# Softmax attention in layer 2: scores by halves, each followed by its banks of maxima

## The chip, the cores and the metric

The kernel runs on one core of a Trainium2 chip. The metric is device time in microseconds (us) of one execution. The engines are called as in the profile: PE is TensorE's matmuls, PEld its weight loads, DVE is VectorE, ACT is ScalarE, POOL is GpSimd and SP is SyncE. PSUM, where matmuls put their results, has eight banks of 512 float32 columns on each of 128 partitions.

## What is computed

The program is a chain of four layers on an array `x` of 2 sequences x 1024 positions x 128 features. Each layer has the form

```python
xn = _layernorm(x, axis=-1)
s = attention_of_the_layer(xn, ...)
g = _silu(ffn_of_the_layer(xn, ...))
x = x + s * g
```

The change is inside the feed-forward branch of layer 2, which itself starts with a causal softmax attention (16 query heads of 8 dimensions, 4 groups of key and value heads, so 4 query heads share one key head):

```python
scores = jnp.einsum('bghsd,bgtd->bghst', Q, K) / jnp.sqrt(jnp.float32(D_K))
mask = jnp.triu(jnp.full((S, S), -1000000000.0, dtype=scores.dtype), k=1)
attn = jax.nn.softmax(scores + mask, axis=-1)
out = jnp.einsum('bghst,bgtd->bghsd', attn, V)
```

A mixture of experts follows it, and layers 0, 1 and 3 hold state-space, delta-rule and expert work that the change leaves alone.

## The kernel before

**Tiling.** A sequence of 1024 is cut into 8 tiles of 128 positions. `steps` lists all pairs of a query tile `sb` and a key tile `tb <= sb` for both sequences: 2 x 36 = 72 steps, numbered from 0. Steps with `tb == sb` are the diagonal ones and need the causal mask. The four head groups lie on the four row groups of the array: group g uses partitions 32g to 32g+31 (`kT[rows]`, `qT[rows]`), so a score matmul contracts over 32 rows, and four of them, one for each group, can stand in the array side by side. Work that uses all 128 rows (the mask matmuls, `pat`, transposes) needs the whole array.

**What a step computes** (`weights`, line 1559). For each group, one matmul writes scores of 128 keys x (4 heads x 128 queries), that is one bank of 512 columns. A second matmul adds the "shift", the negated maximum of each query, kept transposed in `mT`, by multiplying it with ones. In a diagonal step a full-width matmul of `ident` and `nle` puts the mask in first. Groups 0 and 1 share one tile of two banks (`psc`), groups 2 and 3 another. One ACT instruction takes Exp of such a pair of banks into `pr`. A step later `values` multiplies `pr` with the values `va` into the bank `pat`: four matmuls that the profile shows as eight.

**Maxima** (`maxima`, line 1523). The shifts have to exist before a query tile's first step. So every step also computes "banks of maxima" for a later query tile: a tile `pm` of one bank gets scores with queries on the partitions (1 matmul of 512 or 384 columns, 2 of 256, or 4 of 128), and one DVE `tensor_reduce` takes the maxima of it (`mx`). A "masked" bank covers the diagonal keys of one group: a full-width mask matmul (`nge`) first, then 4 matmuls of 128 columns. A "plain" bank needs no mask. `largest` joins the parts into `mp`, `turn` transposes it on PE (`pmt`) and casts it to `mT`. `take` hands out so many banks a step that each tile is done when it is due. By its arithmetic, steps 0 to 37 have five banks (nearly all one masked and four plain), steps 38 to 51 four, 52 to 61 three plain ones, and 62 to 71 none.

**Closing.** When a query tile is done, `close` schedules three small parts into later steps: four transposes of `ao` and a normalisation (`rec`, `at`), one transpose (`patT`), one projection (`pho`). Parts of the next stage (`hidden_columns`, `group_logits`) are put in the same way. All these use `pm` banks and stand at the front of a step.

**Buffers.** The pool `sm` has three banks for `pm` and the small parts, `sc` two tiles of two banks for `psc`, `so` one for `pat`.

**Order.** PE's order in this stage is exactly as written (`manual_schedule` for PE). The other engines' instructions are put in order by the framework's planner, from a model of the time. The written order of one step is:

1. small parts that are due (`run`);
2. mask matmuls of the masked banks (`whole(before)`), and in a diagonal step the `nle` masks of all four groups (the part of `weights` up to its `yield`);
3. the score matmuls of the list `before` (masked banks, filled up with plain ones taken from the end of the step's list, up to three), one matmul of each bank in turn (`rows`);
4. four score matmuls, then four shift matmuls, then the two Exps;
5. the banks of the list `after` (up to three);
6. `values` of the step before.

In a five-bank step with the usual lists that is one masked bank and the plain bank of group 3 ahead of the scores, and the plain banks of groups 0, 1 and 2 behind them.

Every matmul is issued by the helper `K.mm` (line 319), so the profile gives line 319 for all of them, and their tiles tell them apart: `psc<-qT,kT` is a score, `psc<-mT,onesR` a shift, `psc<-nleR,identR` a mask of the step, `pm<-ngeR,identR` the mask of a masked bank, `pm<-kT,qT` a bank of maxima, `pat<-pr,va` the values. `pr<-psc` at line 291 is Exp, `mx<-pm` at line 1535 the reduction.

Of the kernel before, what the change touches and what calls it, by code (L numbers as in the profile page):

```python
# [10 lines left out]
F32 = mybir.dt.float32  # L11
# [8 lines left out]
P = 128  # L20
# [1192 lines left out]
class Dispatch:  # L1213
# [93 lines left out]
    def weights(self, dst, n, rows):  # L1307

        nc = self.K.nc
        e = nc.values_load(self.of[0:1, n : n + 1], engines=[mybir.EngineType.SP], min_val=0, max_val=self.E - 1, skip_runtime_bounds_check_because="a count of experts, at most E - 1")  # L1310
        nc.sync.dma_start(dst, rows[bass.ds(e, 1)].rearrange("e p m -> p (e m)"))
# [122 lines left out]
class Attention:  # L1434
# [73 lines left out]
    def maxima(self, sb, shared, sm):  # L1508

        K, pf, qT, kT = self.K, self.pf, self.qT, self.kT
        nc = K.nc
        four = [P, G, P]
        now = slice(sb * P, (sb + 1) * P)
        mp = shared["mp"][(self.b * TPB + sb) % 4]
        banks = self.banks(sb)
        starts = sorted({a for a, *_ in banks})
        mx = pf.tile([P, len(starts), 4, 4], F32, name=f"mx{len(starts)}", bufs=3)

        def bank(a, m, j, k, g, masked):
            tile = []

            def mask():
                tile.append(sm.tile([P, 512], F32, name="pm", tag="pm"))
                K.mm(tile[0], shared["ident"], shared["nge"], True, False)

            def scores():
                if not masked:
                    tile.append(sm.tile([P, 512], F32, name="pm", tag="pm"))  # L1530
                rows = slice(32 * g, 32 * g + 32)
                for jj in range(k):
                    K.mm(tile[0][:, jj * m : (jj + 1) * m], qT[rows, j + jj, now], kT[rows, a : a + m], not masked, jj == k - 1 or not masked)
                    yield
                nc.vector.tensor_reduce(mx[:, starts.index(a), g, j : j + k], tile[0][:, : k * m].rearrange("p (j m) -> p j m", m=m), AX.X, ALU.max)  # L1535

            return (mask if masked else None), scores

        def largest():
            top = mx[:, 0]  # L1540
            for n in range(1, len(starts)):
                new = pf.tile([P, 4, 4], F32, name="top", bufs=2)
                nc.vector.tensor_max(new, top, mx[:, n])
                top = new
            top = top.rearrange("p g j -> p j g")
            m = mp.rearrange("p j (g r) -> p j g r", r=32)
            nc.vector.tensor_scalar_mul(m[:, :, :, 0], top, -1.0)
            nc.vector.scalar_tensor_tensor(m[:, :, :, 1], top, -1.0, m[:, :, :, 0].bitcast(F32), ALU.mult, ALU.subtract)

        def turn():  # L1550
            pt = sm.tile(four, F32, name="pmt", tag="pm")
            for j in range(4):
                K.mm(pt[:, j, :], mp[:, j, :], shared["ident"])
            self.mT[sb] = pf.tile(four, F32R, name="mT", bufs=4)
            nc.scalar.copy(self.mT[sb], pt)

        return [bank(*b) for b in banks if b[-1]], [bank(*b) for b in banks if not b[-1]], largest, turn

    def weights(self, sb, tb, shared, sc):

        K, qT, kT = self.K, self.qT, self.kT
        scale = float(np.float32(1.0) / np.sqrt(np.float32(8.0)))
        now = slice(sb * P, (sb + 1) * P)
        pair = [P, 2, 4, P]
        psc = [sc.tile(pair, F32, name="psc", tag="ps") for _ in range(2)]
        bank = lambda g: psc[g // 2][:, g % 2]
        rows = lambda g: slice(32 * g, 32 * g + 32)
        if tb == sb:
            for g in range(4):
                K.mm(bank(g), shared["ident"], shared["nle"], True, False)  # L1570
        yield
        for g in range(4):
            K.mm(bank(g), kT[rows(g), tb * P : (tb + 1) * P], qT[rows(g), :, now], tb < sb, False)
        for g in range(4):
            K.mm(bank(g), shared["ones"][rows(g), :], self.mT[sb][rows(g), :, :], False, True)
        self.pr = []
        for ps in psc:
            pr = self.loop.tile(pair, F32, name="pr", bufs=4)
            K.act(pr, ps, AF.Exp, scale=scale)
            self.pr += [pr[:, 0], pr[:, 1]]  # L1580

    def values(self, sb, tb, prs, so):
        if tb == 0:
# [37 lines left out]
def softmax_attention(K, pf, sm, sc, so, seqs, fill):  # L1621

    nc, c = K.nc, K.c
    four = [P, G, P]

    shared = {n: pf.tile(s, F32R, name=n + "R") for n, s in (("ident", [P, P]), ("ones", [P, P]), ("nge", four), ("nle", four))}
    nc.vector.tensor_copy(shared["ident"], c["ident"])
    nc.vector.tensor_copy(shared["ones"], c["ones"])  # L1630
    for n in ("nge", "nle"):
        nc.vector.tensor_copy(shared[n], seqs[0].w[n].unsqueeze(1).to_broadcast(four))
    shared["mp"] = [pf.tile(four, F32R, name=f"mp{n}") for n in range(4)]
    for t in shared["mp"]:
        nc.vector.memset(t.bitcast(F32), 0.0)
    tiles = [(b, sb) for b in range(NB) for sb in range(TPB)]
    steps = [(b, sb, tb) for b, sb in tiles for tb in range(sb + 1)]
    first = [steps.index((b, sb, 0)) for b, sb in tiles]
    plan = []
    for n, (b, sb) in enumerate(tiles):  # L1640
        plan.append(dict(zip(("masked", "plain", "largest", "turn"), seqs[b].maxima(sb, shared, sm))))
        plan[-1]["due"] = first[n] - (2 if n < 3 else 3)
    later = {}
    for s, part in fill:
        later.setdefault(s, []).append(part)

    def take(kind, s, most):

        want = left = 0
        for p in plan:  # L1650
            left += len(p[kind])
            if left:
                want = max(want, -(-left // max(1, p["due"] - s + 1)))
        out = []
        while len(out) < min(want, most):
            p = next(p for p in plan if p[kind])
            out.append(p[kind].pop(0))
        for n, p in enumerate(plan):
            if p["largest"] and not p["masked"] and not p["plain"]:
                ready.append((n, p))  # L1660
        return out

    ready = []

    def run(parts):
        for t in parts:
            if isinstance(t, dict):
                t["turn"]()
                t["turn"] = None
            else:  # L1670
                t()

    def whole(units):
        for full, _ in units:
            if full:
                full()

    def rows(units):
        live = [r() for _, r in units]
        while live:  # L1680
            live = [r for r in live if next(r, r) is not r]

    def finish(s):

        for n, p in ready:
            if p["largest"]:
                assert n < 4 or plan[n - 4]["turn"] is None
                p["largest"]()
                p["largest"] = None
                later.setdefault(max(s + 1, first[n] - 1), []).append(p)  # L1690
        ready.clear()

    def phase(units):
        for a in range(0, len(units), 3):
            whole(units[a : a + 3])
            rows(units[a : a + 3])

    for s in range(-4, 0):
        run(later.pop(s, ()))
        phase(take("masked", s, 99))  # L1700
        phase(take("plain", s, 99))
        finish(s)
    last = None
    for s, (b, sb, tb) in enumerate(steps):
        A = seqs[b]
        before = take("masked", s, 3)
        after = take("plain", s, 6)
        run(later.pop(s, ()))
        room = 3 - len(before)
        extra = after[3:]  # L1710
        after = after[:3]
        before += extra[:room]
        after += extra[room:]
        whole(before)
        w = A.weights(sb, tb, shared, sc)
        next(w)
        rows(before)
        next(w, None)
        rows(after[:3])
        rows(after[3:])  # L1720
        finish(s)
        if last:
            last()

        def last(A=A, s=s, sb=sb, tb=tb, prs=A.pr):
            A.values(sb, tb, prs, so)
            if tb == sb:
                for n, part in enumerate(A.close(sb, sm)):
                    later.setdefault(s + 3 + n, []).append(part)

    last()
    for s in sorted(later):
        run(later[s])
# [211 lines left out]
```

## Time and profile before

| | |
|---|---|
| median of 3 runs | 1346.4 us (1341.18 to 1348.06) |
| the profiled execution's own time | 1351.32 us |
| its span, first to last instruction | 1349.5 us |
| mean granted PE clock over the span | 0.91 |
| PE / DVE / ACT busy in the span | 1154.1 / 870.4 / 507.2 us |
| this stage: first bank of maxima to last Exp | 503.8 to 817.8 us |
| score matmuls / shift matmuls / Exps | 288 / 288 / 144 |
| reductions of maxima | 304 |

Durations in the text come from the profiled execution, whose own time is 4.9 us above the median. In a timeline line the first number is the start in us from the span's start, the second the length of the merged group, `xN` its number of instructions, and square brackets give the engine's idle time before it and what ended it. A line that merges several instructions gives the shape of the first.

### The profile page before, as it was taken

Reading aid. Unit: us, or ns where it says so; the run is one execution under the profiler, and the core shown is the slowest. Engines: PE = TensorE matmul, PEld = TensorE weight load, DVE = VectorE, ACT = ScalarE, POOL = GpSimd, SP = SyncE. Lnnn points to the kernel's source line nnn. Section 1 sums busy time; section 2 is a strip of 40 time slices with the busy share of each in tenths; the row PEclk is TensorE's granted clock in tenths of the full one; section 3 lists DMA queues with packets and bytes.
Section 4 is the critical chain, followed back from the end, with each engine's and each line's share of the span. In section 5 each row is a group of like instructions: output and inputs, shape, how many; then the busy total and the mean of one; then the engine's idle time right before and its main releaser. Section 6 shows DMA issues by size and latency. Waiting matters only on the chain. (4 is left out here: it accounts for less than half of the span.)

```text
span 1349.5 us, 18601 instructions
## 1 busy us (share of the span) xinstructions
PE 1154.1 (86%) x6697; PEld 773.1 (57%) x6697; DVE 870.4 (64%) x2260; ACT 507.2 (38%) x919; POOL 389.9 (29%) x386
## 2 busy tenths in 40 slices
PE   5599977888999288999998995899999378999996
PEld 2267665886996145444444432577778353554555
DVE  7944368946756966777777735877765582363447
ACT  4533335123222241454555674144242244522221
POOL 0073530056642520000000000244775120635430
PEclk9799987899999585999999997799999768999998
DMA  2000003035443000000000000233445311222201
GB/s 90 1 0 1 1 15 125 27 127 156 126 122 97 8 1 0 1 0 1 1 1 17 9 1 8 93 112 117 133 124 142 95 70 33 45 53 62 45 18 32
DMA packets 37803, 71.26 MB, mean 53 GB/s; under 512 B 5275, under 2 KB 22176, under 8 KB 37328
## 3 DMA queue, kind: packets, MB, share of 16 engines
q1 hardware_dynamic: 31408, 55.09, 13.7%
q0 software_dynamic: 5440, 9.79, 3.0%
q10 hardware_dynamic: 864, 5.20, 1.1%
q8 instruction: 53, 0.87, 0.3%
q14 instruction: 38, 0.31, 0.1%
HBM read 62.58 MB, written 8.85 MB: 53 GB/s over the span
## 5 line engine op out<-in xcount | busy, mean ns | idle before, releaser
L1305 POOL DMA_INDIRECT xb<-xs,dfrom x85 | 84.4, 993 | 505.3 <-PE pcum L319 359.7
L1535 DVE TENSOR_REDUCE mx<-pm 128x1 f32<-128x512 f32 (+3 forms) x304 | 181.9, 656 | 63.0 <-PE pm L319 60.5
L291 ACT ACTIVATE pr<-psc 128x1024 f32<-128x1024 f32 x144 | 139.5, 1021 | 99.7 <-PE psc L319 72.6
L319 PE MATMUL pm<-kT,qT 32*128 32x128 f32 (+3 forms) x576 | 119.6, 364 | 15.5 <-DVE mx L1535 11.7
L1315 POOL DMA_INDIRECT ys<-yb,dto x85 | 87.4, 1028 | 82.0 <-DVE yb L1202 50.5
L319 PEld LDWEIGHTS pm<-kT,qT 32*128 32x128 f32 x576 | 69.5, 203 | 69.0 <-DVE mx L1535 48.7
L319 PE MATMUL p<-xbT,tw 128*128 128x256 f32 x368 | 99.3, 386 | 3.8 <-ACT sg L1195 2.6
L325 PE MATMUL tp<-w_c,xn 128*128 128x128 f32 x64 | 20.2, 408 | 72.6 <-DVE xn L369 45.7
L319 PE MATMUL pat<-pr,va 128*32 128x512 f32 x576 | 79.6, 619 | 0.2 <-ACT pr L291 0.2
L1195 ACT ACTIVATE sg<-p,tw 128x256 f32<-128x256 f32 x92 | 41.0, 471 | 91.9 <-PE p L319 74.3
L319 PEld LDWEIGHTS p<-xbT,tw 128*128 128x128 f32 x368 | 62.7, 192 | 14.6 <-ACT sg L1195 4.1
L319 PE MATMUL psc<-qT,kT 32*128 32x512 f32 x288 | 63.7, 487 | 2.8 <-ACT pr L291 2.7
L1196 DVE SCALAR_TENSOR_TENSOR hh<-p,tw,sg 128x256 f32<-128x256 f32 x92 | 42.5, 479 | 33.8 <-ACT sg L1195 22.4
L1875 POOL TENSOR_TENSOR hT<-hT,gb 128x512 f32<-128x512 f32 x32 | 41.2, 1291 | 72.0 <-DVE hT L1873 67.9
L319 PEld LDWEIGHTS po<-tw,hh 128*128 128x128 f32 x368 | 54.4, 192 | 9.3 <-issue 3.8
L1873 DVE TENSOR_TENSOR hT<-hT,put 128x512 f32<-128x512 f32 x36 | 24.5, 685 | 54.5 <-PE put L319 53.1
L325 PEld LDWEIGHTS tp<-w_c,xn 128*128 128x128 f32 x64 | 11.8, 190 | 80.3 <-ACT lnrs L291 46.4
L319 PE MATMUL po<-tw,hh 128*128 128x128 f32 x368 | 56.3, 277 | 0.5 <-DVE hh L1196 0.4
L319 PE MATMUL psc<-mT,onesR 32*128 32x512 f32 x288 | 53.6, 407 | 0.0
L291 ACT ACTIVATE hT<-pgt 128x512 f32<-128x512 f32 x36 | 21.4, 597 | 72.5 <-PE pgt L319 70.0
L605 POOL TENSOR_TENSOR uda<-w_c,vdA 128x512 f32<-128x512 f32 x28 | 28.6, 1039 | 62.4 <-PE pe L319 37.1
L646 DVE TENSOR_TENSOR uxdt<-pt,vdt 128x512 f32<-128x512 f32 x16 | 10.4, 684 | 48.0 <-PE pt L644 47.9
(522 smaller groups left out, 2756.4 us busy)
## 6 DMA issues: line engine op xcount, KB each, us to landing
tw<-in_rows SPq DMA_DIRECT2D x23, 836.0 KB
tw<-in_rows SPq DMA_DIRECT2D x39, 384.0 KB
gb<-gt SPq DMA_DIRECT2D x32, 256.0 KB
yt<-ys SPq DMA_DIRECT2D x16, 256.0 KB
w_l<-in_l ACTq DMA_DIRECT2D x1, 1890.0 KB
w_e<-in_e SPq DMA_DIRECT2D x1, 1536.0 KB
xb<-xs,dfrom POOLq DMA_INDIRECT x85
ys<-yb,dto POOLq DMA_INDIRECT x85
```

What stands on the lines that cost most here:

```text
L291: op = self.nc.scalar.activation(out, in_, func, **kw)
L319: self.nc.tensor.matmul(out, lhsT=lhsT, rhs=rhs, start=start, stop=stop)
L325: self.nc.tensor.transpose(pt[:, j, :], src(g * G + j), self.c["ident"])
L605: pool.tensor_mul(da, upto.unsqueeze(1).unsqueeze(1).to_broadcast(lay), m["dA"][:, i0 + j : i0 + j + per, :].unsqueeze(3).to_broadcast(lay))
L646: nc.vector.tensor_mul(heads(xdt[:, k]), heads(pt), each(m["dt"], k))
L1195: nc.scalar.activation(sg, p1[:, k - k0, :], AF.Silu, bias=t[:, 1536 + k : 1537 + k])
L1196: nc.vector.scalar_tensor_tensor(hh[:, k, :], p2[:, k - k0, :], t[:, 1540 + k : 1541 + k], sg, ALU.add, ALU.mult)
L1305: self.K.nc.gpsimd.indirect_dma_start(dst, None, self.xs, bass.IndirectOffsetOnAxis(self.of_token[:, n : n + 1], 0))
L1315: d = self.K.nc.gpsimd.indirect_dma_start(self.ys, bass.IndirectOffsetOnAxis(self.to[:, n : n + 1], 0), src, None, bounds_check=2 * T - 1, ...
L1535: nc.vector.tensor_reduce(mx[:, starts.index(a), g, j : j + k], tile[0][:, : k * m].rearrange("p (j m) -> p j m", m=m), AX.X, ALU.max)
L1873: nc.vector.tensor_mul(hT, hT, put)
L1875: nc.gpsimd.tensor_mul(hT, hT, gb[k // 2][:, k % 2, :])
```

## The change

`weights` does one half of the groups in a call: half 0 is groups 0 and 1, half 1 groups 2 and 3. A half is its masks (in a diagonal step), its two scores, its two shifts and its Exp. The written order of a step becomes: small parts; mask matmuls of the masked banks; half 0; up to three banks (the masked ones, filled up with plain ones); half 1; the other banks; `values` of the step before. Each unit now carries its group, and the plain banks are sorted so that those of groups 2 and 3 come first. Numbers of instructions, buffers and what `take` hands out stay as they were.

```diff
-            return (mask if masked else None), scores
+            return (mask if masked else None), scores, g
...
-    def weights(self, sb, tb, shared, sc):
+    def weights(self, sb, tb, shared, sc, half):
...
-        psc = [sc.tile(pair, F32, name="psc", tag="ps") for _ in range(2)]
-        bank = lambda g: psc[g // 2][:, g % 2]
+        psc = sc.tile(pair, F32, name="psc", tag="ps")
+        groups = (2 * half, 2 * half + 1)
         rows = lambda g: slice(32 * g, 32 * g + 32)
         if tb == sb:
-            for g in range(4):
-                K.mm(bank(g), shared["ident"], shared["nle"], True, False)
-        yield
-        for g in range(4):
-            K.mm(bank(g), kT[rows(g), tb * P : (tb + 1) * P], qT[rows(g), :, now], tb < sb, False)
-        for g in range(4):
-            K.mm(bank(g), shared["ones"][rows(g), :], self.mT[sb][rows(g), :, :], False, True)
-        self.pr = []
-        for ps in psc:
-            pr = self.loop.tile(pair, F32, name="pr", bufs=4)
-            K.act(pr, ps, AF.Exp, scale=scale)
-            self.pr += [pr[:, 0], pr[:, 1]]
+            for g in groups:
+                K.mm(psc[:, g % 2], shared["ident"], shared["nle"], True, False)
+        for g in groups:
+            K.mm(psc[:, g % 2], kT[rows(g), tb * P : (tb + 1) * P], qT[rows(g), :, now], tb < sb, False)
+        for g in groups:
+            K.mm(psc[:, g % 2], shared["ones"][rows(g), :], self.mT[sb][rows(g), :, :], False, True)
+        pr = self.loop.tile(pair, F32, name="pr", bufs=4)
+        K.act(pr, psc, AF.Exp, scale=scale)
+        self.pr = (self.pr if half else []) + [pr[:, 0], pr[:, 1]]
...
-        before = take("masked", s, 3)
-        after = take("plain", s, 6)
+        masked = take("masked", s, 3)
+        plain = take("plain", s, 6)
         run(later.pop(s, ()))
-        room = 3 - len(before)
-        extra = after[3:]
-        after = after[:3]
-        before += extra[:room]
-        after += extra[room:]
-        whole(before)
-        w = A.weights(sb, tb, shared, sc)
-        next(w)
-        rows(before)
-        next(w, None)
-        rows(after[:3])
-        rows(after[3:])
+        whole(masked)
+        plain.sort(key=lambda unit: unit[2] < 2)
+        room = 3 - len(masked)
+        A.weights(sb, tb, shared, sc, 0)
+        rows(masked + plain[:room])
+        A.weights(sb, tb, shared, sc, 1)
+        rows(plain[room : room + 3])
+        rows(plain[room + 3 :])
         finish(s)
```

The helpers `whole` and `rows` only unpack the third element of a unit.

## The prediction

> **What bounds the stage now.** The edit touches one stage, softmax attention in layer 2, so I first cut the span into stretches (the windows view), setting the borders by the Exp instructions in the timeline.
>
> ```profile
> 532.00:700.70 168.70, 160.86 (x1125) 80.64 (x1122) 127.36 (x252) 86.29 (x111) 0.00 (x0) 0.95 0.00 1
> 700.70:762.50 61.80, 56.22 (x432) 30.28 (x431) 45.94 (x97) 34.63 (x54) 0.00 (x0) 0.97 0.05 14
> 762.50:790.60 28.10, 27.40 (x225) 12.37 (x221) 19.96 (x44) 21.46 (x28) 0.00 (x0) 1.00 0.00 1
> 790.60:822.00 31.40, 27.26 (x188) 9.18 (x186) 2.08 (x6) 21.24 (x26) 0.00 (x0) 1.00 0.00 1
> ```
>
> Columns: length, busy PE, PEld, DVE, ACT, POOL, then clock. The stretches hold steps 0-37 (five banks of maxima each), 38-51 (four), 52-61 (three) and 62-71 (none). PE is nearly always busy, but overlapping matmuls count as busy, so I ask the waits view who stands still in steps 0-51:
>
> ```profile
> PEld pm L319 <- DVE mx L1535: 52.5, 107, 1.5
> DVE mx L1535 <- PE pm L319: 43.1, 46, 4.7
> ```
>
> Each waits for the other: a loop through the three `pm` banks, bound by its latency. One step of it, from the timeline (step 21, PE and then DVE):
>
> ```profile
> 629.68 0.50 PE L319 MATMUL pm<-ngeR,identR 128*128 128x512 f32 x1
> 630.11 0.50 PE L319 MATMUL pm<-kT,qT 32*128 32x128 f32 x2
> 630.12 0.49 PE L319 MATMUL psc<-qT,kT 32*128 32x512 f32 x1
> ...
> 630.46 0.40 PE L319 MATMUL psc<-mT,onesR 32*128 32x512 f32 x1
> ...
> 631.40 1.08 PE L319 MATMUL pm<-kT,qT 32*128 32x512 f32 x2
> 632.41 1.06 PE L319 MATMUL pat<-pr,va 128*32 128x512 f32 x8
> 633.41 0.50 PE L319 MATMUL pm<-ngeR,identR 128*128 128x512 f32 x1
> 630.65 3.08 DVE L1535 TENSOR_REDUCE mx<-pm 128x1 f32<-128x512 f32 x5 [0.66 <-PE pm L319]
> ```
>
> The loop: mask 0.43, first bank to first reduction 0.54 (630.11 to 630.65), two reductions 0.60 + 0.68 (the fifth bank needs the buffer of the second), 0.06 to the fifth bank, 0.41 to `pat`, 1.00 to the next mask: 3.73 us, the distance of the two masks. The eight score and shift matmuls lie under the two reductions.
>
> **Two facts about order.** The second line above shows a score of another row group starting 0.01 us after the first banks, though three masked matmuls stand before it in the written order: a group that is blocked doesn't hold up the others. Signals behave otherwise. Step 34:
>
> ```profile
> 680.50 0.39 PE L319 MATMUL psc<-mT,onesR 32*128 32x512 f32 x2
> ...
> 680.64 0.44 PE L319 MATMUL psc<-qT,kT 32*128 32x512 f32 x1
> ...
> 681.20 1.94 ACT L291 ACTIVATE pr<-psc 128x1024 f32<-128x1024 f32 x2 [1.58 <-PE pm L319]
> ```
>
> Here the masked bank is in group 2, so the shifts of groups 0 and 1, all that the first Exp reads, end at 680.50 + 0.39 = 680.89. The Exp starts at 681.20. What ends at 681.08 is the score of group 2, which stands ahead of those shifts in the written order. In step 21 the last shift itself ends at 631.28 and Exp starts at 631.38, also 0.10 later. I read this as: a matmul's completion is seen only when all written before it have completed.
>
> **Part 1, half 0 moves ahead of the maxima (29 five-bank steps without the diagonal).** New order: mask, scores 0 and 1, shifts 0 and 1, three banks, half 1, two banks, `pat`. The sort puts groups 2 and 3 first, so those banks start beside half 0. But their signals wait for shift 1: score to shift 0.34 (630.12 to 630.46), shift 0.39, reduction 0.04 later (641.36 + 0.44 for a bank, reduction at 641.84): 0.77 instead of 0.54. The loop grows by 0.23. It is not 0.23 everywhere. With 384 columns the second reduction is now another 384-wide one and costs 0.47 instead of the masked bank's 0.60, leaving 0.23 - 0.13 = 0.10. Where DVE is still occupied by `top`, `mp`, `rec` and `at`, or the masked bank is in group 3 (first reduction already 0.65 late), I take 0.05. Sum: 8 x 0.23 + 9 x 0.10 + 12 x 0.05 = +3.3 us; bounds 0 and 29 x 0.23 = +6.7.
> Half 1 (scores, shifts) costs nothing while it lies under the two reductions (0.60 + 0.68 against 0.34 + 0.39); uncovered it would cost 0.73 a step. It stands behind the third bank's buffer wait, and the last two banks and `pat` stand behind it; that wait can grow by over 1 us first. The first Exp comes earlier and the second later, but ACT is idle half the time and `pat` reads probabilities a step old.
>
> **Part 2, nine diagonal five-bank steps.** Four full-width mask matmuls stood before the first bank (0.23 each, 1.07 for four, step 20); now two do. First bank 0.46 earlier, first reduction 0.23 later than that: 9 x -0.23 = -2.1. The other two masks move behind the third bank and need the whole array to drain. In step 20's figures half 1 then ends within 0.05 us of the reductions, so they are just covered; if not, up to 0.46 comes back. Bounds -4.1 and 0.
>
> **Part 3, four-bank steps (ten plain, four diagonal).** The first reduction was the masked bank's, 0.70 after its first matmul (737.35 to 738.05), because it alone preceded the scores; now it comes at 0.77: 10 x 0.07 = +0.7. The diagonal ones gain 0.3 where the masked bank is in group 2 and lose 0.2 where it shares a row group with half 0; I take 0. Bounds -1.6 (first reduction at 0.54 as in step 21: 0.16 a step) and +2.
>
> **Part 4, steps 52-71.** The last stretch repeats every 2.61 us:
>
> ```profile
> 797.78 0.50 PE L319 MATMUL psc<-qT,kT 32*128 32x512 f32 x2
> 798.70 0.50 PE L319 MATMUL psc<-qT,kT 32*128 32x512 f32 x2 [0.41 <-ACT pr L291]
> 798.71 0.72 PE L319 MATMUL psc<-mT,onesR 32*128 32x512 f32 x4
> 799.31 1.02 ACT L291 ACTIVATE pr<-psc 128x1024 f32<-128x1024 f32 x1 [0.67 <-PE psc L319]
> ```
>
> Scores 0 and 1 are done by 798.28, but their shifts queue behind scores 2 and 3, which wait for the second Exp. Hence 1.94 of Exp and 0.67 idle. The new order frees shifts 0 and 1. The gap does not vanish: half 1 waits for that Exp, `pat` (1.03) stands behind half 1, and the next half 0 behind `pat`. This closes over two steps: 0.05 + 0.69 (half 1) + 1.03 + 0.82 (half 0 to its Exp) + 1.84 to 1.94 for two Exps = 4.4 to 4.5, or 2.2 a step. But the closing parts of an output tile (0.59, 0.26 and 0.42 in steps 66-68), until now hidden in the Exp wait, lie on that path. Eight plain steps: 8 x -0.4 = -3.2, +1.3 back, -1.9; two diagonal ones neutral to -0.5. Steps 52-61 have closing parts, logits or transposes on PE in almost every step, and there PE's own sum (0.5 + 0.3 to 1.0 + 1.3 to pass two halves and three banks) stays at 2.4 to 3.1: I take +0.4, since three banks now separate the halves. Sum -1.5; bounds -7 (all 20 gain 0.35) and +1.
>
> **Sum.** 3.3 - 2.1 + 0.7 - 1.5 = +0.4 us. The profiled execution took 1351.3 (span 1349.5); the median of the runs is 1346.4, so 5 lower. I forecast 1347. A difference under about 0.5% (6.7 us) can't be told from none here.
>
> **Against the skill.** The row: a score of another group starts 0.01 us after the first bank, past matmuls written before it (630.12). The Trainium skill, "TensorE: Matmul & The Clock Gate", Part 3, says matmuls are "pc-monotone in start AND end — strict FIFO, no reordering". This case's starts contradict it; the step-34 signal agrees for the ends. By the rule the new first bank would wait for shifts and masked matmuls ahead of it, which is the case C below (1361); by the row it is the sum above.
>
> **Rivals.**
> A, the forecast: gains and losses cancel within 0.5%. 0.44.
> B, faster: signals of different row groups pass one another and the late Exp in step 34 has another cause. Then part 1 is 0, part 2 is -4.1, part 3 is -1.6 and the last steps approach -6: -11.7, so 1335. Against it: the 0.10 us fit in both steps. 0.23.
> C, slower: half 0 really stands in front of the banks. In about half of the steps the masked bank shares group 0 or 1 with half 0; if PE doesn't look past its blocked matmul, the next bank starts at 0.34 + 0.33 instead of 0, and the first reduction comes 0.6 later; in the others 0.3 later. 15 x 0.6 + 14 x 0.3 + 10 x 0.3 = 16.2, less 1.5 of part 4 (part 2 is eaten by the same slip): +14.7, so 1361. It decides once the first reduction slips by over 0.4 us in the five-bank steps (29 x 0.4 = 11.6, less 3.6 of parts 2 and 4, is 8). For it: the new order puts four matmuls of half 0 ahead, two of them blocked. Against it: 630.12 passes three blocked ones. 0.33 with smaller losses of this kind, such as DVE's planned order turning out worse (that order isn't written by hand).
>
> Range: 1336 to 1361, taking in most of B and C; A alone spans 1340 to 1353. Faster by over 0.5% 0.23, within 0.44, slower 0.33.
>
> **What would show it.** In plain five-bank steps the first reduction 0.77 after the first score, and masks 3.9 to 4.0 apart (C: first reduction past 1.1; B: 0.54). In diagonal steps two full-width masks before the first bank, and a period shorter by about 0.2. After step 62 uneven Exp gaps, some zero, averaging 0.3 to 0.6. I am wrong if any of these fails, or if Exp becomes what the banks wait for.

## The result: slower by 1.4%, and the profile after

The changed kernel takes 1365.48 us (median of 4 runs, 1361.24 to 1368.01) beside 1343.79 us for the kernel before in the same comparison: ratio 1.0143, interval 1.0100 to 1.0186. Two later measurements, on two different chips, gave 1.0098 (1.0070 to 1.0126) and 1.0110 (1.0069 to 1.0152). The forecast was 1347 us, no change. Ratios and mean clocks here and in the table below leave out runs more than 1.5% above the fastest of their kernel, six of 172, each at the lowest clock of its kernel; counted in, they would make the clock column -0.0132 for "the change, third", -0.0075 for "shifts late, plain first", -0.0026 for the second "change, more scores" and -0.0032 for the second "change, narrow scores".

The profiled execution's own time is 1363.41 us, its span 1361.6 us (before: 1351.32 and 1349.5). From the start of the first `pm` matmul to the start of the last `pat` matmul the stage takes 334.5 us where it took 315.2: +19.3. The rest of the program is 7 us shorter in this profile than in the one before.

The windows view of the changed kernel (columns: length, busy PE, PEld, DVE, ACT, POOL, PE clock, DMA share, GB/s):

```profile
532.00:700.70 168.70, 161.38 (x1027) 80.50 (x1024) 117.21 (x234) 80.38 (x103) 0.00 (x0) 0.88 0.00 1
700.70:762.50 61.80, 57.13 (x402) 30.65 (x402) 43.21 (x89) 32.26 (x47) 0.00 (x0) 0.94 0.03 9
762.50:790.60 28.10, 26.91 (x203) 14.04 (x200) 19.37 (x41) 17.45 (x26) 0.00 (x0) 0.94 0.04 11
790.60:822.00 31.40, 31.05 (x239) 12.34 (x238) 11.89 (x29) 24.99 (x30) 0.00 (x0) 1.00 0.00 1
```

The borders are those used before, so less work fits: 1027 matmuls in the first stretch instead of 1125. The column to look at is the clock: 0.95 has become 0.88, 0.97 has become 0.94, and 1.00 has become 0.94 in the third stretch. PE is as busy as before.

**Where the clock goes.** The trace gives the granted clock in pieces of 3.41 us, each full or half. Inside the stage 47.8 us were at half clock before and 81.9 us are now. 37.5 us of either lie at the start of the stage; the rest come as single pieces or short series. One series, in the windows view of the changed kernel (20 us ahead of it, the last 3.5 us of these, and the series):

```profile
641.00:661.60 20.60, 19.18 (x155) 9.97 (x154) 15.36 (x34) 11.06 (x14) 0.00 (x0) 1.00 0.01 2
658.10:661.60 3.50, 2.90 (x29) 1.53 (x28) 2.81 (x8) 1.94 (x2) 0.00 (x0) 0.99 0.00 0
661.60:682.00 20.40, 20.40 (x93) 10.40 (x90) 9.60 (x23) 7.40 (x10) 0.00 (x0) 0.50 0.00 1
```

In the series DVE gets 23 instructions done where it got 34 in the 20.6 us ahead. Steps 29 to 32 lie there: 3.48, 3.88, 3.66 and 3.73 us before, 5.53, 6.36, 5.72 and 5.30 after. The same steps and one more in the kernel before, same view:

```profile
661.40:680.00 18.60, 17.74 (x133) 8.30 (x133) 15.26 (x33) 10.92 (x14) 0.00 (x0) 1.00 0.00 1
```

So the loss has two parts. I take a step's period from one step's last `pat` matmul to the next one's, and compare only steps that ran at full clock in both traces:

| steps | forecast each | measured each (steps compared) | in sum |
|---|---|---|---|
| five banks, off the diagonal (29) | +0.11 (3.3 / 29) | +0.215 (17) | +6.2 |
| five banks, diagonal (9) | -0.23 | -0.18 (6) | -1.6 |
| four banks, off the diagonal (10) | +0.07 | +0.175 (9) | +1.8 |
| four banks, diagonal (4) | 0 | -0.04 (2) | -0.2 |
| 52 to 71 and the end | -1.5 in sum | all compared | -0.8 |

That is +5.4 us, the "order sum" from here on (mean change of each kind at full clock, times its steps). The other 13.9 us of the stage's 19.3 stand in steps that touch half clock: 13.9 / (81.9 - 47.8) = 0.41 us lost for each us more at half clock.

**Where the order's part goes.** The waits view between 532.0 and 762.5 us, as before, has a line (the third) that the kernel before had not:

```profile
PEld pm L319 <- DVE mx L1535: 44.5, 86, 3.3
DVE mx L1535 <- PE pm L319: 30.5, 28, 4.1
DVE mx L1535 <- PE psc L319: 20.8, 19, 3.4
```

Reductions now wait 20.8 us, 19 times, for something signalled with a score or shift (`psc`), though they read only `pm`. The timeline of step 21 (PE, then DVE):

```profile
628.78 0.50 PE L319 MATMUL pm<-ngeR,identR 128*128 128x512 f32 x1
629.21 0.50 PE L319 MATMUL psc<-qT,kT 32*128 32x512 f32 x2
629.23 0.49 PE L319 MATMUL pm<-kT,qT 32*128 32x512 f32 x2
629.55 0.39 PE L319 MATMUL psc<-mT,onesR 32*128 32x512 f32 x2
629.78 0.22 PE L319 MATMUL pm<-kT,qT 32*128 32x128 f32 x1
...
632.83 0.50 PE L319 MATMUL pm<-ngeR,identR 128*128 128x512 f32 x1
630.07 3.08 DVE L1535 TENSOR_REDUCE mx<-pm 128x1 f32<-128x512 f32 x5 [0.97 <-PE pm L319]
```

The two plain banks start 0.02 us after the first scores and end at 629.72. Their first reduction starts at 630.07. The shifts of half 0 end at 629.94; the masked bank's first matmul, written behind the shifts and ahead of the plain banks, starts at 629.78, behind half 0 in its own row group, and ends at 630.00. The reduction follows that by 0.07. So it comes 0.86 after the first score, not 0.77, and the masks are 4.05 apart, not 3.73.

The trace shows the signals themselves. All signals of PE in this stage raise one counter, on which the other engines wait, and the trace holds the times at which it is raised. In this step none lies between the end of the plain banks at 629.72 and 629.96; then come 629.96, 630.01, 630.05 and 630.08. That is the written order: shifts, masked bank's first matmul, plain bank, plain bank. The reduction starts 0.02 after the third. By then the plain bank's matmul had been over for 0.33 us.

### The profile page after: what moved, and what is told of

It is laid out like the page before. It is cut to its first block, busy times and chain, and to the rows that moved or that the text cites. A ratio compares the mean times of both kernels' runs of the same rounds, so it can differ in the third digit from the quotient of the medians.

```text
span 1361.6 us, 18599 instructions
## 1 busy us (share of the span) xinstructions
PE 1175.9 (86%) x6697; PEld 789.0 (58%) x6697; DVE 871.1 (64%) x2260; ACT 510.5 (37%) x919; POOL 388.6 (29%) x386
## 5 line engine op out<-in xcount | busy, mean ns | idle before, releaser
L1535 DVE TENSOR_REDUCE mx<-pm 128x4 f32<-128x512 f32 (+3 forms) x304 | 181.1, 655 | 73.6 <-PE pm L319 44.9
L319 PE MATMUL pm<-kT,qT 32*128 32x128 f32 (+3 forms) x576 | 125.0, 377 | 17.2 <-DVE mx L1535 14.8
L319 PEld LDWEIGHTS pm<-kT,qT 32*128 32x128 f32 x576 | 78.0, 210 | 52.9 <-DVE mx L1535 44.9
L319 PE MATMUL pat<-pr,va 128*32 128x512 f32 x576 | 84.6, 660 | 0.0
L325 PE MATMUL tp<-w_c,xn 128*128 128x128 f32 x64 | 20.5, 410 | 72.5 <-DVE xn L369 45.4
L319 PE MATMUL psc<-qT,kT 32*128 32x512 f32 x288 | 79.4, 513 | 0.7 <-ACT pr L291 0.7
L319 PEld LDWEIGHTS p<-xbT,tw 128*128 128x128 f32 x368 | 63.8, 195 | 14.8 <-ACT sg L1195 4.5
L319 PE MATMUL psc<-mT,onesR 32*128 32x512 f32 x288 | 65.0, 409 | 0.0
L319 PEld LDWEIGHTS psc<-qT,kT 32*128 32x128 f32 x288 | 32.4, 193 | 33.8 <-issue 24.7
```

The source lines that it names most:

```text
L319: self.nc.tensor.matmul(out, lhsT=lhsT, rhs=rhs, start=start, stop=stop)
L325: self.nc.tensor.transpose(pt[:, j, :], src(g * G + j), self.c["ident"])
```

## Experiments

In the texts on record "full clock" is a granted clock of 1 in the trace. Every ratio is to runs of the kernel before on the same chip. Clock is the difference of the mean granted clock over the whole span, averaged over the runs compared. It is empty for the first comparison, where the clocks of the runs of the kernel before are not on record. The last three columns come from the one profile of each kernel: the stage's time at half clock, its length minus 315.2, and its order sum. A profile is one draw of the clock. Those of "change, more scores" are of the shortest and the second shortest of 12 runs, that of "plain first, more scores" of the shortest of 6. Those of "the change, again" and "the change, third" are of the longest and the second longest of 6, those of "shifts late, plain first" and "change, narrow scores" of the third or fourth longest of 12. Between these rows the half clock differs by more than the kernels do; the clock column is the fairer one.

| kernel | ratio (interval) | clock | half clock | stage | order sum |
|---|---|---|---|---|---|
| before | 1 | 0 | 47.8 | 0 | 0 |
| the change | 1.0143 (1.0100-1.0186) | | 81.9 | +19.3 | +5.4 |
| the change, again | 1.0098 (1.0070-1.0126) | -0.0099 | 105.8 | +28.5 | +5.7 |
| the change, third | 1.0110 (1.0069-1.0152) | -0.0108 | 105.8 | +27.5 | +4.7 |
| halves adjacent, only without masked bank | 0.9965 (0.9944-0.9986) | +0.0023 | 44.4 | -3.5 | -1.8 |
| change, no sort | 1.0292 (1.0251-1.0333) | -0.0214 | 122.9 | +44.5 | +14.1 |
| change, shifts late | 0.9927 (0.9896-0.9958) | +0.0028 | 37.5 | -7.9 | -3.4 |
| the same, again | 0.9935 (0.9908-0.9961) | +0.0009 | 37.5 | -7.9 | -3.4 |
| shifts late, plain first | 0.9980 (0.9956-1.0004) | -0.0050 | 99.0 | +15.3 | -5.6 |
| before, slower loop | 1.0158 (1.0123-1.0193) | -0.0095 | 85.3 | +24.4 | +14.6 |
| slower loop, more scores | 1.0143 (1.0115-1.0171) | -0.0044 | 61.4 | +18.8 | +14.8 |
| before, more scores | 0.9991 (0.9970-1.0013) | +0.0007 | 47.8 | +1.8 | +0.5 |
| change, more scores | 1.0057 (1.0027-1.0088) | -0.0028 | 44.4 | +4.3 | +6.3 |
| the same, again | 1.0027 (0.9996-1.0058) | 0.0000 | 41.0 | +2.6 | +6.3 |
| change, narrow scores | 1.0054 (1.0028-1.0081) | -0.0035 | 68.3 | +13.6 | +4.2 |
| the same, again | 1.0047 (1.0014-1.0081) | -0.0021 | 64.9 | +13.0 | +6.4 |
| shifts late, more scores | 0.9927 (0.9905-0.9949) | +0.0038 | 47.8 | -2.9 | -2.1 |
| plain first, more scores | 0.9919 (0.9891-0.9948) | +0.0048 | 37.5 | -8.6 | -3.8 |
| the same, again | 0.9957 (0.9933-0.9981) | +0.0005 | 41.0 | -6.9 | -4.1 |
| the same, warmed start | 0.9992 (0.9964-1.0020) | +0.0077 | 20.5 | -1.9 | -3.6 |

In 18 of these 19 profiles (all but the warmed start, which adds work outside the order sum) the stage's change is the order sum plus 0.39 us for each us more at half clock: the correlation of what the order leaves over with the half clock is 0.99. The one miss over 1.5 us is the slower loop (+24.4 measured, +29.2 by the rule). And within the runs of one and the same kernel the time falls by 8.7 us for each 0.01 of mean clock (282 runs, correlation -0.87).

### Which part of the change gains: the last steps alone

```diff
+        if masked:
+            ...            # scores, shifts and banks as in the kernel before
+        else:
+            A.weights(sb, tb, shared, sc, 0)
+            A.weights(sb, tb, shared, sc, 1)
+            rows(plain)
```

> The kernel before, except that steps without a masked bank (52 to 71) run half 0, half 1 and then their plain banks. Theory S (the loss comes from half 0 standing ahead of the first banks in steps 0 to 51, through PE's signals, and from the clock that falls with it): steps 0 to 51 as before, the stage's half-clock time as before (about 48 us), steps 52 to 71 shorter by 2 to 5 us, so 0.2 to 0.4% below before. Rival O (scores and shifts of only two row groups at a time are themselves dear, wherever they stand): steps 52 to 71 gain nothing or lose, time at or above before.

Steps 0 to 51 kept their periods (23 five-bank steps: -0.01 in sum). Steps 62 to 71 changed as in the changed kernel (-3.0 in the plain ones and the end, +1.2 in the two diagonal ones); steps 52 to 61 gained 0.8 and lost 0.85 in the diagonal one. The ratio is 0.9965, some 4.7 us, of which the order sum is 1.8; the mean clock was up by 0.0023 in these runs. So splitting the halves is a small gain in steps 62 to 71, where there are no banks of maxima.

### The sort taken away

```diff
-        plain.sort(key=lambda unit: unit[2] < 2)
```

> The changed kernel without the sort: the first plain banks are those of groups 0 and 1, the row groups of half 0. Theory S (what counts is when the signal of the first bank can come): the first banks now stand behind score and shift in their own row groups, their first reduction comes 1.1 to 1.2 us after the first score instead of 0.85, about 0.3 us a step over some 40 steps: +10 to +14 at full clock, more with the clock, 1375 to 1390. Rival (signals come in the written order anyway, so which group the banks belong to doesn't matter): within 4 us of the changed kernel.

Now the plain banks of groups 0 and 1 come behind half 0, in its own row groups. In step 21 the first reduction comes 1.00 after the first score (1.1 to 1.2 was expected) and the period is 4.20. The order sum is +14.1; the other 30 us of the stage's +44.5 came with 122.9 us at half clock. So the sort is worth a lot to the change.

### Is half 1 in the way: its scores twice

```diff
+        if twice and tb < sb:        # half 1, steps with four or five banks
+            for g in groups:
+                K.mm(psc[:, g % 2], kT[rows(g), tb * P : (tb + 1) * P], qT[rows(g), :, now], True, True)
```

> The changed kernel, with the two scores of half 1 issued twice in steps with four or five banks off the diagonal (the first pair of results is overwritten; outputs unchanged). The extra 0.33 us of PE work lies under the two reductions that the fourth and fifth bank wait for. Theory G (about 14 of the 19 us are clock: the slower loop leaves PE less busy and its clock falls to half more often): half-clock time in the stage falls from 82 us towards 50, and the time by 5 to 14 us against the changed kernel, 1352 to 1360. Rival C (the lower clock in the changed kernel's runs is chance or has nothing to do with how busy PE is): half-clock time about as before the edit, time equal or up to 5 us longer.

> The changed kernel with the full scores of half 1 twice, again, on the same chip as the narrow ones: clock about 0.904 and 1.003 to 1.008 as the first time (theories U and T alike); near 1.012 if the first result was chance.

The periods at full clock stay (step 21: 4.06 against 4.05), so half 1 is covered, as the prediction had it. With more work on PE the kernel is faster than the changed one: 1.0057 and 1.0027, beside 1.0098 to 1.0143 for the changed kernel, which was measured on other chips. Its half clock is 44.4 and 41.0 us, in profiles of two short runs; the mean clock over the runs is down by 0.0028 and 0.0000, where the changed kernel has 0.0099 and 0.0108.

### Does a slower loop alone lose clock

The kernel before, with one more DVE instruction ahead of the first reduction in steps 0 to 51:

```diff
+                if slow[0]:
+                    slow[0] -= 1
+                    idle = pf.tile([P, 192], F32, name="idle", bufs=2)
+                    nc.vector.tensor_copy(idle, tile[0][:, :192])
```

> The kernel before, with one extra DVE copy of 128x192 ahead of the first reduction of each of steps 0 to 51 (the copy goes nowhere). PE's order is that of before; the loop through the banks is slower by the copy's time, about 0.27 us. At full clock that is 46 to 52 steps x 0.27 = 12 to 14 us at most, less where DVE was not on the path: 9 to 13. Theory G (a slower loop makes the clock fall): half-clock time of the stage rises from 48 us to 70 to 100 and the time by 18 to 28 us over before. Rival O (the clock falls because of the order by halves): half-clock time stays near 48 us and the time rises by 9 to 13 only.

The order of PE is untouched here; five-bank steps get 0.26 longer at full clock, and half clock in the stage rises from 47.8 to 85.3 us. The loss of clock isn't special to the change: a longer loop with the same matmuls in it brings it.

### The change once more, and the shifts moved

The shifts of half 0 are written behind the first three banks instead of ahead of them; nothing else differs where there is a masked bank, and steps without one have half 0, half 1, plain banks.

```diff
         for g in groups:
             K.mm(psc[:, g % 2], kT[rows(g), tb * P : (tb + 1) * P], qT[rows(g), :, now], tb < sb, False)
+        yield
...
+            half = A.weights(sb, tb, shared, sc, 0)
+            next(half)
+            rows(masked + plain[:room])
+            list(half)
+            list(A.weights(sb, tb, shared, sc, 1))
```

> The changed kernel again, as the partner of the others on this chip, and for its clock: both theories expect 1.0 to 1.9% above before. Theory G expects a half-clock time in the stage well above the 48 us of before (70 to 100 us); if the first profile was chance, it is 45 to 60 us and the time nearer to 0.5% above before.

> The changed kernel with the two shifts of half 0 written behind the first three banks instead of ahead of them (steps with a masked bank; steps without one run half 0, half 1, plain banks). The banks' matmuls start when they did; only what stands ahead of them in the written order changes. Theory S (a bank's signal waits for everything written ahead of it): the first reduction comes 0.54 to 0.65 us after the first score instead of 0.85, five-bank steps at full clock fall from about 4.05 to 3.73 to 3.85, the half-clock time returns to about 48 us, time at or up to 0.6% below before. Rival O (the pairs of row groups themselves, or the start of the banks, cost the time): first reduction and period stay, time about 1% above before.

> The version with the shifts of half 0 written behind the first three banks, again, beside new runs of the kernel before. Account of two terms (step periods, about -3.4 us here, and some 8 us for each 0.01 of mean granted clock): -3.4 us at a clock equal to that of the kernel before, -6 with +0.003 of clock as the first time; 0.993 to 0.998. If the first result (0.9927) was mostly a lucky clock, 0.998 or above.

Step 21 of the second run of it, timeline of PE, then DVE:

```profile
621.38 0.50 PE L319 MATMUL pm<-ngeR,identR 128*128 128x512 f32 x1
621.81 0.50 PE L319 MATMUL psc<-qT,kT 32*128 32x512 f32 x2
621.82 0.55 PE L319 MATMUL pm<-kT,qT 32*128 32x512 f32 x3
...
625.19 0.50 PE L319 MATMUL pm<-ngeR,identR 128*128 128x512 f32 x1
622.44 3.08 DVE L1535 TENSOR_REDUCE mx<-pm 128x1 f32<-128x512 f32 x5 [0.62 <-PE pm L319]
```

The plain banks start nearly as they did in the changed kernel, 0.01 to 0.06 after the first score. What has changed is what stands ahead of their signals: no shift, only the masked bank's first matmul, which ends at 622.36. The counter is raised at 622.38 and 622.41, and the reduction follows by 0.02, at 622.44. The first reduction comes 0.63 after the first score instead of 0.86, the masks are 3.81 apart instead of 4.05, and the waits view shows the line that was new in the changed kernel nearly gone:

```profile
DVE mx L1535 <- PE psc L319: 2.7, 3, 1.7
```

So the written order of the signals is shown by an edit too, and this kernel beats both others: 0.9927 and 0.9935. The order sum is -3.4. Of it -3.6 come from the nine diagonal five-bank steps and -1.2 from the last steps; five-bank steps off the diagonal stay 0.05 longer than before. The stage's other 4.5 us go with half clock, which is back to the 37.5 us at the stage's start.

### The plain banks ahead of the masked one

```diff
-            rows(masked + plain[:room])
+            rows(plain[:room] + masked)
```

> As the kernel with the shifts written late, but the plain banks of groups 2 and 3 are written ahead of the masked bank. Theory S: now only two scores stand ahead of the first bank, so its reduction comes at 0.54 to 0.58 in nearly all steps (with the masked bank first it is 0.61 to 0.65 where that bank shares group 0 or 1), another 0.05 us a step; with two masks instead of four ahead in diagonal steps, 0.3 to 0.8% below before. Rival (only the shifts' 0.39 us mattered, not the number of matmuls ahead): same as with the masked bank first.

> The kernel before with the extra DVE copy, and the scores of groups 2 and 3 issued twice in steps 0 to 51 off the diagonal (results overwritten, outputs unchanged): the same slower loop, but PE has more to do under the reductions. Theory G: half-clock time falls from 85 us to about 50 and the time from 1.6% above before to 0.7 to 1.1%. Rival C: half-clock time and time as without the extra scores, or longer.

The order is the best of all (-5.6), but the clock took it back: ratio 0.9980, and the single times swing between 1337 and 1362 us as the mean clock swings between 0.910 and 0.883. The profile, of one of the longer runs, has 99.0 us at half clock. Beyond the stage's start the clock falls three times in it, as in the kernel before, but stays down for 20.5, 3.4 and 30.7 us instead of 3.4 each time. So a longer loop isn't the only way to lose clock. The slower loop with extra scores kept its periods (+0.266, as without them) and got a part of its clock back (-0.0044 for -0.0095). In time, 1.0143 can't be told from the 1.0158 without them, where 1.007 to 1.011 was expected.

### More work on PE against the fall of the clock

> The same, and in steps with four or five banks off the diagonal the two scores of half 1 are issued twice (the second overwrites the first with the same values). In two kernels these extra matmuls left the periods of steps at full clock as they were, and the mean clock was 0.004 to 0.013 higher than without them. Theory G (more work on TensorE in these steps lifts the granted clock): clock 0.002 to 0.006 above the run without them, 2 to 5 us shorter, 0.989 to 0.994. Rival N (it was chance): clock and time as without them.

> The version with late shifts and plain banks ahead of the masked one (0.998, mean clock 0.898 against 0.906 of the kernel before, 1337 to 1362 us from run to run), with the scores of half 1 issued twice as above. Step periods at full clock are to stay at about -5 us in sum. Theory G: clock back to 0.904 or more, 1338 to 1342 us, 0.993 to 0.997, and fewer long runs. Rival N: clock near 0.898, 0.997 to 1.001, same spread.

> The version with late shifts, plain banks first and half 1's scores twice, again, beside the one with the warmed start: 0.990 to 0.995 with the clock 0.003 to 0.006 above that of the kernel before, 37.5 us of half clock in the stage.

> The kernel before with the scores of groups 2 and 3 issued twice in steps 0 to 51 off the diagonal, nothing else. They lie under the reductions, so the periods at full clock stay (0 to +0.02 us a step). Theory G: clock 0.002 to 0.005 higher, 0.996 to 0.9985. Rival N: no difference, 0.999 to 1.002.

The same extra scores as above (for the kernel before: of groups 2 and 3). Steps 38 to 51, nearly, in the windows view, first with the plain banks first, then with the extra scores besides:

```profile
690.00:750.00 60.00, 57.91 (x347) 30.94 (x345) 37.85 (x79) 27.66 (x43) 0.00 (x0) 0.74 0.03 10
```

```profile
690.00:750.00 60.00, 57.72 (x461) 31.56 (x454) 45.45 (x99) 35.48 (x56) 0.00 (x0) 1.00 0.05 14
```

PE is busy 96 to 97% of the time in both; the clock is 0.74 and 1.00. These are a long run of the one kernel and the shortest of the other. Over the runs the extra scores move the clock from -0.0050 to +0.0048 and +0.0005 and the ratio from 0.9980 to 0.9919 and 0.9957, on three chips; the last is short of what was expected (0.990 to 0.995, clock +0.003 to +0.006). 0.9919 is the lowest ratio of all, but the shifts-late kernels on the same chip, 0.9935 and 0.9927, can't be told from it. Where there was little half clock beyond the stage's start to win back (before, shifts late) the extra scores change nothing in time that can be told, against the expectation: 0.9991, and 0.9927 beside 0.9935.

### What the clock follows

I counted array use in each piece of 3.41 us: streamed columns times 0.43 ns (0.22 us for 512; masks in a row start 0.23 us apart), times the shares of rows and columns of the array that the matmul uses. Over 20 traces, in the steps (540 to 800 us), half clock begins 66 times: 62 times after a piece with a use below 0.34 (of 271 such pieces), 4 times after one between 0.34 and 0.38 (of 285), never after one above (811). In these traces a low use is thus needed but not sufficient. Two tests of it:

```diff
-                K.mm(psc[:, g % 2], kT[rows(g), tb * P : (tb + 1) * P], qT[rows(g), :, now], True, True)
+                K.mm(psc[0:32, g % 2], kT[rows(g), tb * P : tb * P + 32], qT[rows(g), :, now], True, True)
```

> The changed kernel, in which the extra scores of half 1 (as in the run that issued them twice) use only 32 of the 128 columns of the array: the extra matmul writes 32 partitions instead of 128, streams the same 512 columns through the same 32 rows, and takes the same time. Array use is counted here from the traces as streamed columns x 0.43 ns x rows/128 x columns/128 in one clock window of 3.41 us; over all traces a window below 0.34 may be followed by half clock, one above 0.36 is not. Theory U (array use decides): the extra matmuls add a quarter of what the full ones add (0.007 instead of 0.027 of a window), so the clock stays near that of the changed kernel, 0.890 to 0.898, ratio 1.009 to 1.014, over 60 us of half clock in the stage. Theory T (busy time of TensorE or the streamed columns decide): as with the full extra scores, clock about 0.904, ratio 1.003 to 1.008, under 50 us.

> The changed kernel, unchanged, as the missing control of the narrow extra scores on the same chip: mean clock 0.008 to 0.012 below that of the kernel before, ratio 1.009 to 1.014 as in two earlier measurements. If this clock loss itself varies from chip to chip, nearer to 0.004 and 1.005.

> The narrow extra scores of half 1, beside the changed kernel without them. If rows times columns decide (theory U): clock within 0.003 of the changed kernel, time the same within 3 us. If the busy time of TensorE or the streamed columns decide (theory T): clock 0.005 or more above it, 1.003 to 1.007 against the kernel before, 5 to 8 us shorter than the changed kernel.

On the chip where both ran, the changed kernel has 1.0110 and a clock 0.0108 down, with the narrow scores 1.0047 and 0.0021 down; the two intervals just overlap. The narrow scores lift the clock nearly as the full ones do. Theory T's prices hold and U's do not, except that the single profiles with narrow scores show 64.9 and 68.3 us of half clock where T had under 50; they are of long runs, those with full scores of short ones. So rows times columns, though it sorts the pieces well, is probably not what decides here. I tried other counts on the same pieces, some 1350. A limit that takes in all 66 falls takes in 471 pieces by array use, 421 by streamed columns times rows, 572 by PE's busy time and 724 by streamed columns alone. Columns times rows would fit the narrow scores too, but no run tests it; and why the plain banks' place matters to the clock stays open.

```diff
                 if not masked:
                     tile.append(sm.tile([P, 512], F32, name="pm", tag="pm"))
+                    for _ in range(warm[0]):        # 2 before step 0, then 0; the same ahead of the masks
+                        K.mm(tile[0], shared["ident"], shared["nge"], True, True)
```

> The version with late shifts, plain banks first and half 1's scores twice (0.9919), and besides, in the stage's start-up before step 0, each bank of maxima is preceded by two full-width mask matmuls whose results are overwritten. There the first window holds an array use of 0.17 and is followed by 37.5 us of half clock, in all kernels so far. Theory U: the use rises by about 0.3 in these windows, the half clock ends early or never begins: under 20 us of half clock in the stage, 0.985 to 0.990, if the extra matmuls (48 of 0.22 us, partly under reductions) cost less than 4 us. If array use isn't what ends the half clock: still 30 us or more of it, and 0.993 to 1.000 with the cost of the extra matmuls.

```profile
500.00:516.10 16.10, 13.81 (x76) 8.61 (x74) 9.13 (x18) 1.14 (x2) 0.34 (x2) 1.00 0.00 0
516.10:533.10 17.00, 16.42 (x48) 9.95 (x48) 5.31 (x9) 0.59 (x1) 0.00 (x0) 0.50 0.00 1
```

The windows view of this kernel: the first 13 us of the stage (from 502.5) keep the full clock, where the others fall to half after 2 to 4 us and stay there for 24 to 44 us, and half clock in the stage falls to 20.5 us. But the time is not better (0.9992, beside 0.9957 without it on that chip). From the first `pm` matmul to the end of the first `pat` matmul it takes 44.2 us, where the three other kernels of this order take 36.7 to 37.0. The extra matmuls weren't hidden: this stretch got 7 us longer in spite of its higher clock.

## Why the prediction was wrong, step by step

**The step that failed: the sum had no term for the clock.** The prediction showed the clock column (0.95, 0.97) and priced everything at the durations of steps at full clock. 13.9 of the 19.3 us that the stage lost in the profile go with 34.1 us more at half clock. The later runs agree: a clock lower by 0.0099 and 0.0108, at 8.7 us for each 0.01, is 8.6 and 9.4 us; with the order sums of 5.7 and 4.7 that makes 14.3 and 14.1 us, or 1.05%, where 0.98% and 1.10% were measured. So the clock is about three fifths of the loss or more. That a longer loop alone brings such a loss is shown by the kernel before with the slower loop: +0.26 us a step, clock -0.0095. A sum of the right size without the clock, +5.4, would have been 0.4%, inside "no change". The runs with more scores show the same from the other side: the change's order, with its clock mostly restored, costs 0.3 to 0.6%.

**Part 1, right in kind, too small.** Signals in written order decide, as it said. The term of 0.77 let the reduction follow the last shift by 0.04. It missed the signals in between: `rows` writes the masked bank's first matmul behind the shifts and ahead of the plain bank, and the counter is raised for one after the other, 0.034 us apart. In step 22 of the changed kernel the masked bank is in group 2, off the row groups of half 0, and its first matmul is done at 633.60, well before the shifts (634.00). Still the counter is raised at 634.02, 634.05 and 634.09 and the reduction starts at 634.11, 0.84 after the first score. Where the masked bank shares a row group with half 0, as in step 21, it is 0.86. In steps with 384 columns the old value was 0.48, not 0.54 (step 22), so these grew by 0.23 and not by 0.10. Together with the small value assumed for 12 of the 29 steps (0.05) that made +0.11 a step where +0.215 was measured; in sum 6.2 us, within the bound of 6.7.

**Part 2** held: -0.18 for -0.23. **Part 3** took +0.07 where +0.175 came, from the same place: with the shifts written late it is +0.01. **Part 4**: the plain last steps, with the end, gained 3.1 us where -1.9 was forecast, but the two diagonal ones lost 0.58 each (forecast: neutral or better), and steps 52 to 61 gave +1.1 for +0.4; in sum -0.8 for -1.5. The uneven Exp gaps came as described, in the timeline of ACT:

```profile
811.17 1.02 ACT L291 ACTIVATE pr<-psc 128x1024 f32<-128x1024 f32 x1 [0.28 <-PE psc L319]
812.83 3.85 ACT L291 ACTIVATE pr<-psc 128x1024 f32<-128x1024 f32 x4 [0.64 <-PE psc L319]
817.89 1.94 ACT L291 ACTIVATE pr<-psc 128x1024 f32<-128x1024 f32 x2 [1.22 <-PE psc L319]
```

**Rivals.** B (signals pass one another) is out: the counter is raised in the written order, and the shifts' place in it moved the first reduction by 0.23 us while the plain banks' starts stayed. C came near the time (1361) by a mechanism that did not occur: the banks of the other row groups start 0.02 us after the first score, past blocked matmuls, and the first reduction is at 0.86, not past 1.1.

**Against the skill.** The start at 629.23, ahead of matmuls written before it, again contradicts the "strict FIFO" of the Trainium skill, "TensorE: Matmul & The Clock Gate", Part 3, for starts. For ends, the signals at 629.96 to 630.08 agree with it; the profile's modelled end of the plain bank (629.72), ahead of that of an earlier-written matmul (630.00), does not.

The Trainium skill, "TensorE: Matmul & The Clock Gate", Part 1, explains the clock by a gate of two states, full and half, decided in free-running windows of about 3.4 us, and its table of the two states has it fall after an idle window. The two states and the 3.41 us agree with these traces; that condition does not. In the 3.50 us ahead of the half clock of 661.60 PE was busy for 2.90 us, so no window there was idle, and by the table the clock's share of this loss would have been zero. The same Part tells of a kernel whose clock swings because PE idles briefly and often between groups of matmuls, which is nearer to this case, but gives no limit or price for it.

## What to carry to other kernels

Price the clock: where a stage shows a granted clock below 1 now and then (here 0.95), some 0.2 us more in a loop of 3.7 us can cost more than twice its own sum, and redundant matmuls in an array that waits anyway can pay. For every wait find the last matmul written ahead of its signal, not only the one that it reads: moving two shifts behind three banks turned +1.0% into -0.7% on the chip where both ran.

## What the runs showed of the hardware that was not expected

- PE's clock falls to half within a stage in which PE counts as busy 95% of the time; a us at half clock costs this stage 0.39 us.
- PE raises its counter in the written order of the matmuls, also across row groups, and in none of the 20 traces twice within less than 0.034 us.
- Redundant matmuls give clock back to the changed kernel, and 32 of the array's 128 columns are nearly as good for it as all: -0.0108 without, -0.0021 with narrow ones on one chip; -0.0035 with narrow and 0.0000 with full ones on another.
- The mean clock of one and the same kernel differs from run to run by 0.022 and more (the change with more scores: 0.895 to 0.917, 1370 to 1351 us), so a single profile shows one draw of it.
